# Graph attention on one core: gathered rows that carry their own ones, runs of seven chunks, three scratch writes

## The chip, the cores and the metric

The kernel runs on one core of a Trainium2 chip. The metric is the device time of one launch in microseconds; for the kernel before it is 7131.07 us, the median of three runs (7125.32 to 7133.75). Five engines work side by side and meet at semaphores: PE (matrix products), DVE (VectorE, elementwise work and reductions), ACT (ScalarE, activations and copies), POOL (GpSimd, which here issues the indirect gathers) and SP (SyncE, which issues the plain transfers).

## What is computed

A graph network on 6250 nodes (128 features) and 200,000 edges, sorted by destination `dst`. The destinations are drawn as `6250 * u**2`, so low nodes have many edges and high nodes few. Two convolutions are followed by an attention layer; the part that matters here is the attention:

```python
q = (h @ qw + qb).reshape(n, H, HD)          # H = 8 heads of HD = 16
k = (h @ kw + kb).reshape(n, H, HD)
v = (h @ vw + vb).reshape(n, H, HD)
logits = (q[dst] * k[src]).sum(-1) * scale + (edge_attr @ ew + eb)
amax = segment_max(logits, dst)
pe = exp(logits - amax[dst])
ssum = segment_sum(pe, dst)
w = pe / clip(ssum[dst], 1e-06)
o = segment_sum(w[:, :, None] * v[src], dst)
o = group_norm(o.reshape(n, D) @ ow + ob, an_g, an_b)
return h + o                                  # the caller adds x
```

Each convolution gathers a row for every edge's source, adds a row for its destination and a term of the edge, normalises, applies SiLU, and sums over the destination.

## The kernel before

**Chunks.** The edges are cut into 196 chunks of 1024 (128 partitions by `NT` = 8 columns). All three layers (`conv(1)`, `conv(2)`, and the attention from L1154 on) loop over these chunks with the same driver, `pipeline` (L713). It also writes out, by `in_order` (L701), that DVE, SP, ACT and PE execute in program order; POOL has only its own order.

**The gather.** For each chunk `gather` (L620) issues eight indirect DMAs on POOL (L622), one for each column of 128 edges. In a convolution a row is 128 floats of `b_d`; in the attention it is `KV` = 256 floats of `kv_d` (L39), k and then v, in DRAM. After the eight gathers of a chunk come `REST[i]` writes of a scratch tile `nst2` on POOL (L634): three in a convolution, four in the attention (L28). The next chunk's gathers are ordered behind the last of these writes.

**One attention step, n.** `fetch(n+1)` (L1305) issues the loads and gathers of chunk n+1 into a buffer `g` from a pool of `G + 3` = 11. `second` (L1328) finishes one earlier chunk: it builds the one-hot matrix on DVE (`onehot`, L637), adds the sums of a chunk before (`add_late`, L1292), forms weighted v (`weighted`, L1239: ACT copies `pe` to a seventeenth column behind each head of a tile `v`, DVE multiplies v by `pe`), lets ACT put the maxima `wl` and an end flag `ef` behind it (L1346, L1347), and lets PE sum by destination (`sums`, L1248). Then `first(n)` (L1315) multiplies the gathered k by q (`logits`, L1182; L1187 is the DVE instruction that waits for the gather), and `products` (L1312) lets PE make q for chunk n+1.

**Runs.** The maxima over edges of one destination are found for a run of `G` = 8 chunks at once (`maxima`, L1205): PE transposes, DVE scans twice forward over 512 columns (L1219) and once backward over 1024 (L1222), PE transposes back, DVE subtracts (L1230) and ACT makes `pe`. `spread` (L327) cuts the 196 chunks into runs: the last three have 6, 4 and 2 chunks, the first takes the remainder, all others have `G`. That is 26 runs before. A chunk's `second` comes after its run's maxima, so a chunk lives for a whole run and a little more in its `g` buffer.

**Finishing nodes between chunks.** `plan_batches` (L352) fixes the steps at which a batch of four windows of 128 nodes is finished while the chunks go on (`attention_nodes`, L870), at most 40 of the 49 windows (`NWD` = 40). For each planned step it notes a chunk number, three less than the seconds done so far; on the chip the windows already closed at that chunk are read from the first destination of the chunk (`batches`, L377). The end of each batch is the smaller of the last end plus four and that number of windows. What of the 40 windows is not reached by the last batch is done after the pipeline in `mend` (L643): `to_mend` (L405) makes the count of batches `(43 - last) >> 2`, and a loop around two inner loops runs if it is above zero. `last_nodes` (L935) then does windows 40 to 48.

**Where k and v come from.** In the second convolution `conv_nodes` (L804) writes k and v of four windows to `kv_d` by one DVE addition each (L861) and one transfer each (L858).

Of the kernel before, what the change touches and what calls it, by code (L numbers as in the profile page):

```python
# [8 lines left out]
FP = mybir.dt.float32  # L9
# [3 lines left out]
ALU = mybir.AluOpType  # L13
# [8 lines left out]
P = 128  # L22
D = 128
H = 8
HD = 16
NT = 8
CH = NT * P
REST = {1: 3, 2: 3, 3: 4}  # L28
G = 8
GC = 2  # L30
BN = 4
LG = 2
# [3 lines left out]
DB = D + H  # L36
PITCH = D + 4
VK = H * (HD + 1)
KV = 2 * D  # L39
EPS = 1e-5  # L40
BIG = 1e30
PAD_DST = 1 << 20
# [3 lines left out]
def kernel(ctx: ExitStack, tc: tile.TileContext, x, src, dst, eat, w, out):  # L46
# [9 lines left out]
    nc = tc.nc  # L56
# [295 lines left out]
    def plan_batches(i):  # L352

        ends, todo = steps_of(i)
        out, done = [], 0
        for n, now in enumerate(todo):
            done += len(now)
            if n % 8 == (4 if i == 3 else 1) and n > (40 if i == 3 else 80) and n + 6 < NCH \
                    and (i == 3 or n + 5 in ends):
                out.append((n, max(done - 3, 0)))  # L360
        return out if NWD else []

# [441 lines left out]
    def conv_nodes(b, i, w, m, idle=0):  # L804


        at = span(w, m)
        c = b.pool.tile([P, 2, BN], FP, name="n_c")
        if i == 1:
            nc.vector.tensor_scalar(c[:, 0, :m], U[:, at, D], 1.0, None, ALU.max)  # L810
            nc.vector.tensor_scalar(c[:, 1, :m], U[:, at, D], 1.0, None, ALU.min)
            nc.vector.reciprocal(c[:, 0, :m], c[:, 0, :m])
            nc.vector.tensor_copy(cnt[:, :, at], c[:, :, :m])
        else:
            nc.vector.tensor_copy(c[:, :, :m], cnt[:, :, at])
        st = b.tile(m, "x")
        nc.vector.tensor_tensor(st, U[:, at, :D], c[:, 0, :m, None].to_broadcast([P, m, D]), ALU.mult)
        yield
        tT = b.turned(st, m)
        yield  # L820
        o = b.times(tT, m, squares[f"c{i}_w2"])
        yield
        A = b.tile(m, "A")
        for j in range(m):
            nc.vector.scalar_tensor_tensor(
                A[:, j, :], rows[f"c{i}_b2"], c[:, 1, j:j + 1], o[:, j, :], ALU.mult, ALU.add)
        sq = b.squares_of(A, m)
        yield
        nc.vector.tensor_reduce(b.var(), sq, AX.X, ALU.add)
        yield "root"  # L830
        b.scaled(A, m, f"n{i}_g", f"n{i}_b")
        yield
        nc.scalar.activation(A, A, AF.Silu)
        yield
        if i == 1:
            nc.vector.tensor_tensor(A, A, temb[:, None, :].to_broadcast([P, m, D]), ALU.add)
        else:
            nc.vector.tensor_tensor(A, A, h0[:, at, :], ALU.add)
        yield

        for _ in range(idle):
            yield
        if i == 2:
            nc.sync.dma_start(out=rows_of(h2_d, w, m), in_=A)
        tT = b.turned(A, m, "t")
        yield
        if i == 1:
            ends = ((wab[2][:, D:], None, b_d[2]), (wab[2][:, :D], None, a_d[2]))
        else:
            ends = ((qkv_t[:, 1, :], "kb", kv_d[:, :D]), (qkv_t[:, 2, :], "vb", kv_d[:, D:]),  # L850
                    (qkv_t[:, 0, :], "qb", a_d[3]))
        done = None
        for rhs, bias, d_ in ends:
            o = b.times(tT, m, rhs)
            if bias:
                yield
            if done:
                nc.sync.dma_start(out=rows_of(done[0], w, m), in_=done[1])  # L858
            t = b.tile(m, "o")
            if bias:  # L860
                nc.vector.tensor_tensor(t, o, rows[bias][:, None, :].to_broadcast([P, m, D]), ALU.add)  # L861
            else:
                nc.scalar.copy(t, o)
                yield
            done = d_, t
        if bias:
            yield
        nc.sync.dma_start(out=rows_of(done[0], w, m), in_=done[1])
# [291 lines left out]
    with ExitStack() as es:  # L1160
        pool = lambda n, b, **kw: es.enter_context(tc.tile_pool(name=f"{n}a", bufs=b, **kw))
        pools = {"oh": pool("oh", 2), "ps": pool("ps", 1, space=PSUM)}
        gp, wk, vp = pool("gp", G + 3), pool("wk", 2), pool("vp", 1)
        ps_ = pools["ps"]
        iota = ps_.tile([P, D], FP, name="iota")
        nc.vector.tensor_copy(iota, iota_j)
# [71 lines left out]

        def weighted(k):  # L1239

            k.v = vp.tile([P, NT, VK + H + 1], FP, name="v")
            v4 = k.v[:, :, :VK].rearrange("p t (h c) -> p t h c", c=HD + 1)
            nc.scalar.copy(v4[:, :, :, HD], k.pe)
            nc.vector.tensor_tensor(
                v4[:, :, :, :HD], k.g[:, :, D:].rearrange("p t (h c) -> p t h c", c=HD),
                k.pe[:, :, :, None].to_broadcast([P, NT, H, HD]), ALU.mult)

        def sums(k, wide):  # L1248
            k.u = ps_.tile([P, 512], FP, name="u", tag="u", bufs=2)
# [45 lines left out]
        class Stage:  # L1295
            ahead = 1
            sums, late, nb = [], [], None
            lg, j = None, 0

            def __init__(self, bp):  # L1300
                self.bp = bp
# [2 lines left out]

            def fetch(self, c):  # L1305
                k = loads(c, pools, a_d[3], self.ahead)
                k.g = gp.tile([P, NT, KV], FP, name="g")
                gather(k, k.g, kv_d, REST[3])
                k.qe = []
                return k  # L1310

            def products(self, k):  # L1312
# [2 lines left out]
            def first(self, k):  # L1315
                if self.j == 0:
                    self.lg = wk.tile([P, NT, G, H], FP, name="lg")
                logits(k, self.lg[:, :, self.j, :])
                self.j += 1

            def reduce(self, k):
                pass
# [5 lines left out]
            def second(self, run, ks):  # L1328


                pieces = iter(())
                if run:
                    pieces = maxima(run, self.lg, self.nb, self.bp)
                    self.nb, self.j = None, 0
                for n, k in enumerate(ks):
                    mine = pieces if n == len(ks) - 1 else iter(())
                    next(mine, None)
                    onehot(k, pools, iota)
                    next(mine, None)


                    if self.late:
                        add_late(self.late.pop(0))
                    next(mine, None)
                    weighted(k)
                    nc.scalar.copy(k.v[:, :, VK:VK + H], k.wl)  # L1346
                    nc.scalar.copy(k.v[:, :, VK + H], ef[:, k.c * NT:(k.c + 1) * NT])  # L1347
                    sums(k, VK + H + 1)
                    if self.sums:
                        merge_late(self.sums[0])  # L1350
                        self.late.append(self.sums.pop())
                    self.sums.append(k)
                for _ in pieces:
                    pass

            def batch(self, j):
# [17 lines left out]
        def left(k):  # L1374
            lp = pools["left"]
            left_rows(k, pools, a_d[3], "qe", [P, TB, DB], 3)
            k.g = gp.tile([P, NT, KV], FP, name="g")
            gather(k, k.g, kv_d)
            k.qe = []
            products(k, [(k.ohf.rearrange("p t e -> p (t e)"), k.rows), (k.ea, webl)])  # L1380
            lg = lp.tile([P, NT, H], FP, name="l_lg")
            logits(k, lg)
            neg = lp.tile([P, 4, P], FP, name="l_neg")
            part = lp.tile([P, H, 2], FP, name="l_part")
            junk = lp.tile([P, 4, P], FP, name="l_junk")
            for a in range(2):
                nc.vector.tensor_scalar(neg, k.ohf[:, 4 * a:4 * a + 4, :], 1.0, BIG, ALU.subtract, ALU.mult)
                for h in range(H):
                    bc = ps_.tile([P, 4, P], FP, name="l_bc", tag="blk")
                    for t in range(4):  # L1390
                        nc.tensor.transpose(bc[:, t, :], lg[:, 4 * a + t, h:h + 1].to_broadcast([P, P]), ident)
                    nc.vector.tensor_tensor_reduce(
                        junk, bc, neg, 1.0, -BIG, ALU.add, ALU.max, part[:, h, a:a + 1])
            cm = lp.tile([P, H], FP, name="l_cm")
            nc.vector.tensor_reduce(cm, part, AX.X, ALU.max)
            me = ps_.tile([P, NT, H], FP, name="l_me", tag="pe")
            for t in range(NT):
                nc.tensor.matmul(me[:, t, :], lhsT=k.ohf[:, t, :], rhs=cm, start=True, stop=True)
            nc.vector.tensor_tensor(lg, lg, me, ALU.subtract)

            nc.vector.tensor_scalar(lg, lg, 0.0, None, ALU.min)
            k.pe = lp.tile([P, NT, H], FP, name="l_pe")
            nc.scalar.activation(k.pe, lg, AF.Exp)
            weighted(k)
            sums(k, VK)
            tt = t3[:, bass.ds(k.win, 1), :]
            merge(k, M[:, bass.ds(k.win, 1), :], None, cm[:, None, :], 1)
            add(k, tt, 1)
# [43 lines left out]
```

## Time and profile before

| what | value |
|---|---|
| median of the runs | 7131.07 us |
| the profiled execution | 7126.42 us |
| its span, first to last instruction | 7124.6 us |
| granted TensorE clock, mean | 0.723 |
| POOL busy | 5394.0 us (76%) |
| DVE busy | 5144.2 us (72%) |
| PE busy | 3891.3 us (55%) |
| ACT busy | 3308.5 us (46%) |
| attention, first gather | 4669.4 us into the span |
| attention, end of the pipeline on DVE | 7098.6 us |

The profile names a line, an engine and an operation with its output and inputs, a count, the busy time of the group, the mean duration of one, and the idle time of the engine before it with what ended that idle time. Register, branch, semaphore and DMA-issuing instructions are not counted as busy, and a transfer appears as a wait of whoever needs it. The indirect gathers on POOL do show a duration: it is the time that POOL takes to issue one, not the time until it lands.

### The profile page before, as it was taken

What the parts mean: (1) busy time and instruction counts of PE and PEld (TensorE: products, weight loads), DVE (VectorE), ACT (ScalarE), POOL (GpSimd) and SP (SyncE); (2) the same over time, 40 slices, a digit from 0 to 9 for tenths busy, and PEclk for the clock granted to TensorE, in tenths of its full rate; (3) what the DMA queues carried; (4) which work ended last, traced back from release to release, by engine and by line L of the source; (5) the groups of instructions that cost most, each with busy time, mean ns of one, the idle gap of its engine ahead of it and who ended that gap; (6) DMA issues with size and microseconds to landing.
All of it is one profiled execution on the core that took longest, in us unless ns stands there. A gap on an engine that the chain in (4) does not pass through costs nothing. (4 is left out here: it accounts for less than half of the span.)

```text
span 7124.6 us, 74065 instructions
## 1 busy us (share of the span) xinstructions
PE 3891.3 (55%) x20957; PEld 3685.5 (52%) x20958; DVE 5144.2 (72%) x7564; ACT 3308.5 (46%) x5293; POOL 5394.0 (76%) x6678
## 2 busy tenths in 40 slices
PE   5555555555555455555555555545555555555555
PEld 4555555555555455555555555535555555555554
DVE  7777777777777576667777777736667777777778
ACT  5555555555555555555555555522223333333332
POOL 5777777777777677777777777767777777777774
PEclk7776677777777666666777777767777777777777
DMA  5433333333333333333333333344455555555553
GB/s 148 117 97 91 94 110 92 100 100 100 95 100 89 91 90 94 95 94 89 101 107 106 100 106 106 86 130 132 131 146 140 141 142 140 141 146 141 138 139 89
DMA packets 414321, 800.44 MB, mean 112 GB/s; under 512 B 101813, under 2 KB 274984, under 8 KB 379496
## 3 DMA queue, kind: packets, MB, share of 16 engines
q0 software_dynamic: 175616, 411.34, 22.2%
q1 hardware_dynamic: 232646, 380.69, 19.0%
q10 hardware_dynamic: 5632, 3.51, 0.2%
q8 instruction: 172, 2.82, 0.2%
q14 instruction: 255, 2.09, 0.1%
HBM read 754.19 MB, written 40.96 MB: 112 GB/s over the span
## 5 line engine op out<-in xcount | busy, mean ns | idle before, releaser
L622 POOL DMA_INDIRECT g<-b_d,src_i x3136 | 3000.7, 957 | 978.7 <-issue 940.0
L1030 PE MATMUL u<-h,oh 128*128 128x129 f32 (+1 forms) x6272 | 1395.6, 412 | 1891.2 <-ACT h L1025 1891.2
L1030 PEld LDWEIGHTS u<-h,oh 128*128 128x128 f32 x6272 | 1290.1, 314 | 1971.5 <-ACT h L1025 1963.9
L622 POOL DMA_INDIRECT g<-kv_d,src_i x1568 | 1532.4, 977 | 500.9 <-issue 468.8
L1251 PE MATMUL u<-v,oh 128*128 128x145 f32 x3136 | 750.0, 425 | 767.2 <-DVE nm L1284 765.6
L1251 PEld LDWEIGHTS u<-v,oh 128*128 128x128 f32 x3136 | 698.5, 308 | 801.9 <-issue 801.9
L1000 PE MATMUL m<-pk,ohT 117*128 117x128 f32 x6272 | 973.7, 321 | 134.9 <-DVE h L1006 101.1
L1006 DVE TENSOR_TENSOR h<-m,g 128x1024 f32<-128x1024 f32 x392 | 479.0, 1222 | 762.3 <-DMA g<-b_d,src_i 750.4
L1000 PEld LDWEIGHTS m<-pk,ohT 117*128 117x128 f32 x6272 | 942.0, 237 | 162.1 <-DVE h L1006 126.9
L1025 ACT ACTIVATE h<-h 128x1024 f32<-128x1024 f32 x392 | 414.2, 1057 | 1182.9 <-DVE h L1024 1182.9
L634 POOL MEMSET nst<- 128x392 f32 x1960 | 842.7, 430 | 79.3
L1008 ACT ACTIVATE sq<-h 128x1024 f32<-128x1024 f32 x392 | 413.9, 1056 | 653.8 <-DVE h L1006 650.8
L1009 DVE TENSOR_REDUCE var<-sq 128x64 f32<-128x1024 f32 x392 | 477.7, 1219 | 314.8 <-ACT sq L1008 312.2
L1187 DVE TENSOR_TENSOR g<-qe,g 128x384 f32<-128x384 f32 (+1 forms) x588 | 293.8, 511 | 549.7 <-DMA g<-kv_d,src_i 510.1
L615 ACT ACTIVATE ohT<-ohT,minus_p 112x1024 f32<-112x1024 f32 x588 | 669.9, 1139 | 16.2 <-DMA ohT<-rel_d 16.0
L616 ACT ACTIVATE ohT<-ohT 112x1024 f32<-112x1024 f32 x588 | 621.4, 1057 | 18.7
L1178 PE MATMUL qe<-pk,ohT 117*128 117x136 f32 x3136 | 512.8, 319 | 165.5 <-ACT ebs L1188 159.3
L1178 PEld LDWEIGHTS qe<-pk,ohT 117*128 117x128 f32 x3136 | 474.1, 225 | 198.8 <-ACT ebs L1188 192.3
L1023 DVE TENSOR_TENSOR h<-h,cps 128x1024 f32<-128x1024 f32 x392 | 478.4, 1220 | 13.5
L1024 DVE TENSOR_TENSOR h<-h,cps 128x1024 f32<-128x1024 f32 x392 | 478.4, 1220 | 13.4
L1020 DVE TENSOR_TENSOR h<-h,cps 128x1024 f32<-128x1024 f32 x392 | 475.3, 1212 | 5.9
L639 DVE TENSOR_TENSOR oh<-cps,dm 128x1024 f32<-128x1024 f32 x392 | 475.9, 1214 | 0.0
(265 smaller groups left out, 4383.9 us busy)
## 6 DMA issues: line engine op xcount, KB each, us to landing
ohT<-rel_d SPq DMA_DIRECT2D x294, 896.0 KB
g<-b_d,src_i POOLq DMA_INDIRECT x3136
pk<-a_d SPq DMA_DIRECT2D x588, 56.0 KB
g<-kv_d,src_i POOLq DMA_INDIRECT x1568
ohT<-in_eat_dram SPq DMA_DIRECT2D x294, 40.0 KB
a_d<-n_o SPq DMA_DIRECT2D x28, 256.0 KB
kv_d<-n_o SPq DMA_DIRECT2D x28, 256.0 KB
n_h<-h_d SPq DMA_DIRECT2D x19, 256.0 KB
```

Of the source, the lines that this page charges most:

```text
L615: nc.scalar.activation(k.ohT[:WN, :], k.ohT[:WN, :], AF.Square, bias=minus_p[:WN])
L616: nc.scalar.activation(k.ohT[:WN, :], k.ohT[:WN, :], AF.Relu, bias=1.0, scale=-4.0)
L622: return nc.gpsimd.indirect_dma_start(out=g[:, t, :table_d.shape[1]], out_offset=None, in_=table_d, in_offset=bass.IndirectOffsetOnAxis(ap ...
L634: last = nc.gpsimd.memset(nst2, 0.0)
L1000: nc.tensor.matmul(k.m[:, t, :], lhsT=lhs[:, t * P:(t + 1) * P], rhs=rhs, start=(j == 0), stop=(j == len(terms) - 1))
L1006: nc.vector.tensor_tensor(k.mt, k.m, k.g, ALU.add)
L1009: return lambda: nc.vector.tensor_reduce(var[:, j * NT * H:(j + 1) * NT * H], sq.rearrange("p t (g c) -> p (t g) c", c=HD), AX.X, ALU.add)
L1023: nc.vector.tensor_tensor(k.mt, k.mt, over_edges(gam), ALU.mult)
L1024: nc.vector.tensor_tensor(k.mt, k.mt, over_edges(bet), ALU.add)
L1030: nc.tensor.matmul(k.u[:, :wide], lhsT=k.oh[:, t, :], rhs=k.h[:, t, :wide], start=(t == 0), stop=(t == NT - 1))
L1178: nc.tensor.matmul(qe[:, t, :], lhsT=lhs[:, e], rhs=rhs, start=(j == 0), stop=(j == len(terms) - 1))
L1251: nc.tensor.matmul(k.u[:, :wide], lhsT=k.oh[:, t, :], rhs=k.v[:, t, :wide], start=(t == 0), stop=(t == NT - 1))
```

## The change

Five things are done together.

- `KV` becomes 128 + 136: a row of `kv_d` holds k and then, for each head, 16 values of v and a one. `conv_nodes` writes the v half from a tile `n_v` of 136 columns, with a memset for the ones and one DVE addition for each window in place of one for all.
- `weighted` multiplies these 136 columns by `pe` inside the gathered tile `g`, which has nine columns more for `wl` and `ef`. The separate tile `v` and ACT's copy of `pe` go, and ACT puts `ef` in place when the chunk is fetched.
- Runs have 7 chunks in place of 8 (30 runs in place of 26), and the pool of `g` has `G + 4`, which is again 11.
- The attention's scratch writes go from four to three for each chunk.
- The last part of `maxima` (subtraction, `exp`, `wl`) moves behind the logits of the step (`rest`), the second forward scan and the backward one move behind `sums`, and a batch starts three steps after the end of a run, 20 batches in place of 19.

```diff
-REST = {1: 3, 2: 3, 3: 4}
-G = 8
+REST = {1: 3, 2: 3, 3: 3}
+G = 7
-KV = 2 * D
+KV = D + VK
@@ plan_batches
-            if n % 8 == (4 if i == 3 else 1) and n > (40 if i == 3 else 80) and n + 6 < NCH \
-                    and (i == 3 or n + 5 in ends):
+            if n > (40 if i == 3 else 80) and n + 6 < NCH and (
+                    n - 3 in ends and n + 3 not in ends if i == 3 else n % 8 == 1 and n + 5 in ends):
                 out.append((n, max(done - 3, 0)))
@@ conv_nodes
+            if bias == "vb":
+                t = b.pool.tile([P, BN, VK], FP, name="n_v")[:, :m, :]
+                v4 = t.rearrange("p w (h c) -> p w h c", c=HD + 1)
+                nc.vector.memset(v4[:, :, :, HD], 1.0)
+                for j in range(m):
+                    nc.vector.tensor_tensor(
+                        v4[:, j, :, :HD], o[:, j, :].rearrange("p (h c) -> p h c", c=HD),
+                        rows[bias].rearrange("p (h c) -> p h c", c=HD), ALU.add)
+                done = d_, t
+                continue
@@ attention
-        gp, wk, vp = pool("gp", G + 3), pool("wk", 2), pool("vp", 1)
+        gp, wk, vp = pool("gp", G + 4), pool("wk", 2), pool("vp", 1)
@@ weighted
-            k.v = vp.tile([P, NT, VK + H + 1], FP, name="v")
+            k.v = k.g[:, :, D:]
             v4 = k.v[:, :, :VK].rearrange("p t (h c) -> p t h c", c=HD + 1)
-            nc.scalar.copy(v4[:, :, :, HD], k.pe)
             nc.vector.tensor_tensor(
-                v4[:, :, :, :HD], k.g[:, :, D:].rearrange("p t (h c) -> p t h c", c=HD),
-                k.pe[:, :, :, None].to_broadcast([P, NT, H, HD]), ALU.mult)
+                v4, v4, k.pe[:, :, :, None].to_broadcast([P, NT, H, HD + 1]), ALU.mult)
@@ fetch
-                k.g = gp.tile([P, NT, KV], FP, name="g")
+                k.g = gp.tile([P, NT, KV + H + 1], FP, name="g")
                 gather(k, k.g, kv_d, REST[3])
                 k.qe = []
+                nc.scalar.copy(k.g[:, :, KV + H], ef[:, c * NT:(c + 1) * NT])
@@ Stage.first
                 logits(k, self.lg[:, :, self.j, :])
                 self.j += 1
+                self.rest()
@@ Stage.second
                     next(mine, None)
                     onehot(k, pools, iota)
-                    next(mine, None)
                     if self.late:
                         add_late(self.late.pop(0))
                     next(mine, None)
                     weighted(k)
                     nc.scalar.copy(k.v[:, :, VK:VK + H], k.wl)
-                    nc.scalar.copy(k.v[:, :, VK + H], ef[:, k.c * NT:(k.c + 1) * NT])
                     sums(k, VK + H + 1)
+                    next(mine, None)
...
-                for _ in pieces:
+                self.pieces = pieces
+                if run and run[-1].c == NCH - 1:
+                    self.rest()
+
+            def rest(self):
+                for _ in self.pieces:
                     pass
```

More of the change, by code (lines that the diff above doesn't have):

```diff
@@ L1297 @@
             sums, late, nb = [], [], None
-            lg, j = None, 0
+            lg, j, pieces = None, 0, iter(())
             def __init__(self, bp):
@@ L1376, in left @@
             left_rows(k, pools, a_d[3], "qe", [P, TB, DB], 3)
-            k.g = gp.tile([P, NT, KV], FP, name="g")
+            k.g = gp.tile([P, NT, KV + H + 1], FP, name="g")
             gather(k, k.g, kv_d)
```

## The prediction

> **What bounds the kernel now.** I read the page first (POOL 76%, DVE 72% of the span: no verdict), then the attention alone by groups, then the waits, then the order of time on POOL. The change lies almost wholly in the attention, from 4669 to 7099 us. The groups of that stretch, then DVE's waits from 4700 to 7040 us:
>
> ```profile
> L622 POOL DMA_INDIRECT g<-kv_d,src_i x1547 | 1512.5, 978 | 475.8 <-issue 463.0 <-DVE g L1187 5.4 <-DVE wl L1234 4.2
> L634 POOL MEMSET nst<- 128x392 f32 x776 | 333.2, 429 | 33.6
> ```
> ```profile
> DVE g L1187 <- DMA g<-kv_d,src_i: 484.9, 304, 8.6
> ```
>
> POOL's idle time before gathers is 0.30 us each and nearly all "issue": it waits for nobody. DVE waits 485 us for gathers. One chunk of POOL is 8 x (0.978 + 0.30) + 4 x (0.429 + 0.04) = 12.1 us, and 196 of these are 2375 us; the stretch of the gathers, 4669 to 7051, has 2382. So POOL's own instructions set the pace, and the scratch writes are on the path. In order of time, first with three writes (second convolution), then with four:
>
> ```profile
> 4604.38 0.94 POOL L622 DMA_INDIRECT g<-b_d,src_i  x1 [0.30 <-issue]
> 4605.31 1.41 POOL L634 MEMSET nst<- 128x392 f32 x3
> 4607.02 0.95 POOL L622 DMA_INDIRECT g<-b_d,src_i  x1 [0.30 <-issue]
> ```
> ```profile
> 5341.70 0.94 POOL L622 DMA_INDIRECT g<-kv_d,src_i  x1 [0.30 <-issue]
> 5342.64 1.89 POOL L634 MEMSET nst<- 128x392 f32 x4
> 5344.83 0.95 POOL L622 DMA_INDIRECT g<-kv_d,src_i  x1 [0.30 <-issue]
> ...
> 5352.34 2.86 POOL L622 DMA_INDIRECT g<-kv_d,src_i  x1 [0.30 <-issue]
> ```
>
> Three writes take 1.41 us, four 1.89. The last row is a gather three times as long as its neighbours; on DVE the backward scan of a run lies over it:
>
> ```profile
> 5352.15 2.28 DVE L1222 TENSOR_TENSOR_SCAN fw<-nbe,fw 64x1024 f32<-64x1024 bf16 x1
> ```
>
> The gather starts 0.19 us after the scan and ends 0.77 us after it, 1.9 us late. That happens about once in a run.
>
> **DVE's reserve.** Its time not spent waiting for gathers is 2340 - 485 = 1855 us for 192 chunks (the count of L1190 there), 9.65 us a chunk against POOL's 12.1.
>
> **The change, part by part.**
>
> *Fourth write:* 195 gaps between chunks x 0.48 us = **-94 us**, as long as DVE stays below POOL.
>
> *Runs of 7:* 30 runs for 26. Four more backward scans stall a gather by 1.9 us each: **+8 us**. The Trainium skill (SBUF — State Buffer, Who interferes with whom) has two-input DVE instructions contend only with GpSimd instructions that read SBUF, and infers that issuing transfers is spared; that would make this term 0. The row above shows the stall, so I take 8. Since the scans now come later in the step, a stall could also fall on the scratch writes: between -45 (all of the present stalls gone, 24 x 1.9) and +15.
> On DVE a run costs 2.28 + 2 x 1.24 + 0.68 + 8 x 0.21 = 7.1 us whatever its length but for a few tenths: per chunk 0.89 becomes 1.0. A batch costs about 6.9 us (ten instructions of 0.2 to 0.69), one for 7 chunks and not 8: +0.12.
>
> *Weighted v in place:* 1088 elements for 1024, at 1.21 us for 1024 about +0.08 us a chunk. ACT loses the copy of `pe` (0.258 us). DVE's sum is 9.65 + 0.11 + 0.12 + 0.08 = 10.0 us a chunk, against POOL's 12.1 - 0.48 + 0.1 = 11.7. The reserve of 1.7 us hides these; without cover they would cost 0.31 x 196 = 61 us.
>
> *Longer life of `g`:* it is now released by PE's sums, not by `weighted`; a shorter run gives a step back. Chunk c takes the buffer of c - 11, whose second came one step before the fetch and now comes two before. POOL waits for no buffer now and should not afterwards: 0. If it did, all eight gathers of the chunk and the writes behind them would queue, and DVE's L1187 would wait for them. The `ef` copy moves ahead in ACT's order, past the copies of the earlier chunks; it waits for the same release, two steps old: 0. If it instead waited for the gather landing in the same tile, `compared` and the copies of `wl` behind it would wait, and PE's sums with them. Against that, ACT's L1346 (columns 136 to 143 of `v`) starts at 7058.65 while DVE's write of the other columns only starts at 7058.85: columns of one tile are not ordered.
>
> *Longer rows:* 1056 bytes for 1024. POOL's price for a gather is the unknown that matters. Both ends from one view, attention then convolution (512-byte rows):
>
> ```profile
> L622 POOL DMA_INDIRECT g<-kv_d,src_i x1539: 942/946/2936, 4699.2 to 7038.0; - x193
> ```
> ```profile
> L622 POOL DMA_INDIRECT g<-b_d,src_i x3025: 938/944/2424, 199.9 to 4599.4; - x190
> ```
>
> Doubling the bytes added 2 ns to the median; 32 more add nothing on this row. The other end is a row cut in two, which could double the issue: +0.95 us. I take 0. The transfer: the Trainium skill (DMA: Bandwidth & Descriptors, How a descriptor splits into AXI transactions) says that a piece of HBM not starting on 256 bytes is fetched from the boundary below. 1024 bytes are 32 beats; 1056 at a pitch of 1056 are 33 to 40, on average an estimated 36.5, 14% more. This rule speaks against the change: the gathers' queue has 31.9% of engine time from 5300 to 7000 us, so 4.5% of 2382 us, 107 us, if that were the path. The row says it isn't (DMA share 0.51 in all): 0, and some tenths on the last landing.
>
> *k and v rows in the second convolution:* one addition of 0.68 us becomes a memset and four of about 0.27 (the 128-wide rows of L825). The 10 batches lie under POOL there, too. The three groups at its end don't: 0.2 + 3 x 0.27 - 0.56 = 0.45 each, +1.4 us. The tail of the attention saves the 1.1 us that L1244 waits for ACT's copy. Together **+1 us** with the longer multiplications.
>
> *Batches and `mend`:* what is late next. By the rule of the plan, the old last batch starts at step 188 and looks at chunk 179. With dst = 6250 u² over 200,000 sorted edges, its first edge is at u = 179 x 1024 / 200,000 = 0.916, node 5250, window 41: capped at 40, nothing is left. The new last batch starts at 180 (step 187 fails, as a run ends at 190) and looks at chunk 170: u = 0.870, node 4735, window 36. Hence (43 - 36) >> 2 = 1: the loop of `mend`, skipped now, runs one batch, with nothing beside it. Its price is not in this trace. The batch alone, from the rows of the attention's batches: DVE 0.20 + 0.35 + 0.69, PE 1.06, ACT 0.59, PE 1.05, DVE 0.68, ACT 0.63, DVE 0.68, ACT with its table load 1.60, DVE 0.35 + 0.69 + 2 x 0.69 + 0.69 + 0.69 = 12.0, the store about 3 until landed: 15 us. Passing one loop is seen once here:
>
> ```profile
> 7098.14 0.44 DVE L1276 TENSOR_TENSOR flat<-flat,u 128x272 f32 x1
> 7103.27 0.36 DVE L874 TENSOR_SCALAR n_rec<-flat 128x24 f32<-128x24 f32 x3 [4.70 <-DMA n_h<-h_d]
> ```
>
> 4.7 us. The taken path passes the skipped inner loop, the batch loop's end and the outer loop's end beside that: 2 to 6 passages, 9 to 28 us. I take 18, between the ends because the loop's end must also await its transfers: **+33 us**, bounds 24 to 43.
>
> Also one more batch under POOL, +1. Sum: -94 + 8 + 1 + 33 + 1 = **-51 us**: the span goes from 7124.6 to about 7074, the profiled execution from 7126.4 to 7075. The median lies 4.7 us above that execution: 7131 - 51 = **7080 us**.
>
> **The rivals.**
>
> *The DVE becomes the bound.* Runs of 7 bring a step of maxima or of a batch oftener, and a step of maxima takes some 16 us. Were the chain of waits to need the whole 11.7 us and 0.2 more, POOL would wait for buffers and the gain would be 94 - 0.2 x 196 = 55: 7080 + 39 = 7119. For it: DVE has no gap over a tenth in steps with maxima. Against: 1.7 us of reserve a chunk.
>
> *The gather gets dearer* (the slower side). One mechanism: L622's issue grows with the odd row length. Each 0.1 us costs 1568 x 0.1 = 157 us: 7237. It decides from 51 / 1568 = 33 ns a gather. For it: rows are no longer a power of two, and no such gather is in the trace. Against: 944 and 946 ns.
>
> *The change does more than I count:* the scans' stalls fall on the writes and `mend` costs 24: 7080 - 53 - 9 = 7018; half of the stalls gone, 7050.
>
> **How the numbers follow.** Likeliest, POOL bound with `mend`: 0.70, 7055 to 7105. Stalls gone or `mend` cheap: 0.09. DVE bound: 0.10, 7105 to 7130. Dearer gather: 0.11. The range 7048 to 7112 holds the first, most of half-gone stalls, and a little of the DVE case. A measurement of this kernel can tell about 0.2%, 14 us, from no change: faster (below 7117) 0.85, same 0.04, slower 0.11.
>
> **What would show it.** Right: POOL's triples of writes take 1.41 us in the attention, gathers stay at 946 ns median, 30 long gathers beside L1222, DVE's waits for gathers fall from 2.5 to about 1.7 us a chunk, and between the last `add_late` and `last_nodes` a lone batch of L874 to L907 takes some 33 us. Wrong: gathers whose idle time ends with PE u or DVE v (buffers), a median above 980 ns, or no lone batch.

## The result, and the profile after

The changed kernel takes **7053.03 us** (median of 4 runs, 7051.68 to 7058.71), the kernel before beside it 7130.90 (7125.32 to 7133.75): a ratio of 0.9893, 95% interval 0.9876 to 0.991. That is 78 us less by the medians and 73.3 by the spans of the two profiled executions (7124.6 and 7051.3). Forecast were 51.

Where the 73.3 us went is read from five moments in each trace:

| moment, us into the span | before | after | stage's change |
|---|---|---|---|
| first gather of the attention | 4669.4 | 4666.6 | -2.8 |
| last gather of the attention | 7050.1 | 6960.6 | -86.7 |
| end of the pipeline on DVE | 7098.6 | 7004.7 | -4.4 |
| first instruction of `last_nodes` | 7103.3 | 7028.9 | +19.5 |
| end of the span | 7124.6 | 7051.3 | +1.1 |

The gathers' stretch first. The gather is now L623, the write L635, the instruction that waits for the gather L1198. The groups of the attention (busy us, mean ns, idle time before them and what ended it), then DVE's wait for gathers from 4700 to 6930 us:

```profile
L623 POOL DMA_INDIRECT g<-kv_d,src_i x1568 | 1522.4, 971 | 519.1 <-issue 472.2 <-PE u L1261 24.1 <-ACT ebs L1199 8.0
L635 POOL MEMSET nst<- 128x392 f32 x588 | 253.4, 431 | 22.6
```
```profile
DVE g L1198 <- DMA g<-kv_d,src_i: 368.5, 180, 7.3
```

588 writes are three for each of 196 chunks. A gather issues as fast as before (its median is 947 ns). DVE still waits for gathers, 368.5 us in 190 chunks, 1.9 a chunk against 2.5: POOL still sets the pace. New is the end of the first row: PE and ACT now end some of POOL's idle time. In order of time on POOL:

```profile
5340.95 1.40 POOL L635 MEMSET nst<- 128x392 f32 x3
5342.74 0.95 POOL L623 DMA_INDIRECT g<-kv_d,src_i  x1 [0.39 <-issue]
...
5354.23 0.95 POOL L623 DMA_INDIRECT g<-kv_d,src_i  x1 [0.39 <-issue]
5355.49 2.38 POOL L623 DMA_INDIRECT g<-kv_d,src_i  x1 [0.31 <-issue]
```

The triple takes 1.40 us in place of 1.89, but the gather behind it starts after 0.39 us, not 0.30. Gather to gather across a chunk's end the median went from 3.13 to 2.74 us, 0.39 less and not 0.48. The last row is a gather held up by the backward scan, which is L1233 here and runs from 5354.83 to 5357.11: the gather ends 0.76 us after it.

Where the time before a chunk's first gather comes from is seen at the start of the attention, where the first eleven chunks take fresh buffers. The last such chunk and one of the next two, before and then after:

```profile
4787.92 0.95 POOL L622 DMA_INDIRECT g<-kv_d,src_i  x1 [0.16 <-issue]
...
4799.81 0.95 POOL L622 DMA_INDIRECT g<-kv_d,src_i  x1 [0.30 <-issue]
```
```profile
4781.00 0.95 POOL L623 DMA_INDIRECT g<-kv_d,src_i  x1 [0.15 <-issue]
...
4805.17 0.95 POOL L623 DMA_INDIRECT g<-kv_d,src_i  x1 [0.39 <-issue]
```

A fresh buffer costs the same in both kernels. From the twelfth chunk on POOL must ask whether a used one is free, and this costs 0.14 us before and 0.24 after.

Second, the end. DVE between the last `add_late` (L1286) and `last_nodes` (the last row):

```profile
7004.30 0.44 DVE L1286 TENSOR_TENSOR flat<-flat,u 128x272 f32 x1
7011.56 0.18 DVE L885 TENSOR_SCALAR n_rec<-flat 128x32 f32 x1 [6.82 <-DMA n_xr<-in_x_dram]
...
7023.35 0.69 DVE L913 TENSOR_TENSOR n_A<-n_A,n_xr 128x512 f32<-128x512 f32 x1
7028.85 0.35 DVE L885 TENSOR_SCALAR n_rec<-flat 128x24 f32<-128x24 f32 x3 [4.81 <-issue]
```

This is the lone batch that the prediction expected, with 6.8 us to enter the loop, 12.5 of work and 4.8 to leave.

### The profile page after: what moved, and what is told of

It reads as the page before. It is cut to its first block, busy times and chain, and to the rows that moved or that the text cites. A ratio compares the mean times of both kernels' runs of the same rounds, so it can differ in the third digit from the quotient of the medians.

```text
span 7051.3 us, 75298 instructions
## 1 busy us (share of the span) xinstructions
PE 3858.6 (55%) x21045; PEld 3643.6 (52%) x21046; DVE 5182.3 (73%) x7700; ACT 3300.5 (47%) x5111; POOL 5296.6 (75%) x6482
## 5 line engine op out<-in xcount | busy, mean ns | idle before, releaser
L623 POOL DMA_INDIRECT g<-b_d,src_i x3136 | 2996.0, 955 | 977.8 <-issue 942.4
L623 POOL DMA_INDIRECT g<-kv_d,src_i x1568 | 1522.4, 971 | 519.1 <-issue 472.2
L1261 PE MATMUL u<-g,oh 128*128 128x145 f32 x3136 | 694.3, 402 | 666.5 <-issue 640.6
L1261 PEld LDWEIGHTS u<-g,oh 128*128 128x128 f32 x3136 | 645.1, 287 | 709.7 <-issue 701.8
L635 POOL MEMSET nst<- 128x392 f32 x1764 | 760.1, 431 | 68.0
L1019 ACT ACTIVATE sq<-h 128x1024 f32<-128x1024 f32 x392 | 413.8, 1056 | 646.5 <-DVE h L1017 641.9
L1198 DVE TENSOR_TENSOR g<-qe,g 128x384 f32<-128x384 f32 (+1 forms) x588 | 285.0, 511 | 431.3 <-DMA g<-kv_d,src_i 396.6
L1034 DVE TENSOR_TENSOR h<-h,cps 128x1024 f32<-128x1024 f32 x392 | 478.4, 1221 | 13.5
```

Source lines behind the costliest of these rows:

```text
L623: return nc.gpsimd.indirect_dma_start(out=g[:, t, :table_d.shape[1]], out_offset=None, in_=table_d, in_offset=bass.IndirectOffsetOnAxis(ap ...
L635: last = nc.gpsimd.memset(nst2, 0.0)
L1034: nc.vector.tensor_tensor(k.mt, k.mt, over_edges(gam), ALU.mult)
L1261: nc.tensor.matmul(k.u[:, :wide], lhsT=k.oh[:, t, :], rhs=k.v[:, t, :wide], start=(t == 0), stop=(t == NT - 1))
```

## The experiments

**Theory.** POOL's own instructions set the pace before and after. The dropped write is worth nearly the whole gain, and the rest of the change adds or takes a few tens of microseconds where nothing lies beside it. **Rival.** The write alone can't be dropped: with runs of 8 and the old step, DVE and PE have no reserve, and it is the other parts that let POOL run at the shorter pitch.

Three jobs of four kernels were run, each on one chip and beside the kernel before. In the first job the kernel before took 7333.74 us (7313.71 to 7371.33, 23 runs) at a granted clock of 0.69 to 0.70, in the second and third 7130.54 and 7130.57 us at 0.72 to 0.73. The first and the third ran on a chip of the same number, so it isn't known whether another chip or another condition of the same one made the first job slow. Its times are compared only within it; those of the other two may stand side by side.

### First job: four parts, under the slower condition

*The longer rows alone.* The kernel before with rows of 1056 bytes, written in `conv_nodes` as in the change; tile `v` stays.

```diff
-KV = 2 * D
+KV = D + VK
...
-                v4[:, :, :, :HD], k.g[:, :, D:].rearrange("p t (h c) -> p t h c", c=HD),
+                v4[:, :, :, :HD], k.g[:, :, D:].rearrange("p t (h c) -> p t h c", c=HD + 1)[:, :, :, :HD],
```

> The kernel before with rows of 1056 bytes alone: v stands in the row with a one behind each head, but the tile v, ACT's copy of pe, runs of 8 and four writes stay. Theory (the issue of a gather doesn't depend on the length of the row, and the transfer is hidden): within 5 us of 7131, gathers at a median of 946 ns, the share of the gathers' queue up from 31.9% to about 36%. Rival (the odd row length has a price that the rest of the change hides): 20 us or more above 7131, from 13 ns a gather on.

Measured: 7340.90 us (12 runs), ratio 0.9996 (0.9979 to 1.0014); median gather 949 ns. The row length costs nothing that can be seen. The rival of a dearer gather is out. The gap across a chunk's end is 3.14 us, as before (3.13), so the longer rows are not what lengthened POOL's start of a chunk either.

*The fourth write back in the changed kernel.*

```diff
-REST = {1: 3, 2: 3, 3: 3}
+REST = {1: 3, 2: 3, 3: 4}
```

> The kernel after with the fourth scratch write put back in the attention, nothing else. Theory: a pitch of about 12.0 us a chunk by the median (11.51 + 0.49), so +90 us against after, 7053 to about 7140, and no better than before: all of the gain hangs on the one write. Rival (rows, order and shorter runs bring a part of the gain by themselves): below 7110.

Measured: 7356.19 us (10 runs), ratio 1.0033 (1.0016 to 1.005). With four writes the changed kernel is a little slower than the kernel before: its other parts together gain nothing. Its gap across a chunk's end is 3.22 us for 3.14 in the kernel of the rows alone: the dearer asking is there with four writes, too.

*The fourth write dropped from the kernel before, nothing else.*

```diff
-REST = {1: 3, 2: 3, 3: 4}
+REST = {1: 3, 2: 3, 3: 3}
```

> The kernel before with one edit: three scratch writes a chunk in the attention and not four; runs of 8, tile v and rows of 1024 bytes stay. Theory (POOL's own instructions set the pace, a write costs 0.49 us of POOL in each of 195 gaps): about -94 us, 7130 to 7037, with POOL's pitch of a chunk at a median of 11.40 us, so faster than the whole change. Rival (the shorter runs and the step of lead are what make a third write's removal possible; with runs of 8 DVE or the buffers hold POOL back): -40 us or less, and POOL's idle time before gathers ends with a DVE instruction.

Measured: 7478.50 us (4 runs), ratio **1.0191** (1.0163 to 1.022). Slower: under this condition the theory falls. Its waits from 4700 to 6900 us:

```profile
ACT v L1243 <- remote: 211.8, 70, 7.2
POOL g L622 <- DVE cm L1287: 199.2, 43, 8.4
DVE fw L1219 <- remote: 104.7, 18, 10.5
```

POOL now waits for DVE, 43 times and up to 8.4 us, and DVE and ACT wait for something that the profile can put down to no instruction or transfer of the core ("remote"). One such place, just after PE's transposes of a run:

```profile
5284.92 0.28 PE L1216 MATMUL lt<-ident,lg 128*64 128x128 f32 x1 [1.14 <-issue]
...
5289.48 1.21 DVE L1219 TENSOR_TENSOR_SCAN fw<-nbs,lt 64x512 f32<-64x512 bf16 x1 [5.68 <-remote]
```

Four such transposes take 1.06 us together at 5290.75, for the next half. Here the last of them ends, by the trace (which models the ends of PE's products), at 5285.2, and the scan that reads them starts 4.3 us later.

*The lone batch taken away from the changed kernel*, by last runs of 5, 4 and 2 chunks, so that the plan reaches window 40.

```diff
-        sizes, n = ([2, 4, 6], G) if i == 3 else ([1, 1], GC)
+        sizes, n = ([2, 4, 5], G) if i == 3 else ([1, 1], GC)
```

> The kernel after with the last three runs of 5, 4 and 2 chunks in place of 6, 4 and 2. The steps at which nodes are finished move, the last one starts at step 188 and reaches window 40, so the loop after the pipeline is passed over. Theory (the lone batch costs 24.1 - 4.7 = 19.4 us): 7053 to about 7033. Rival (the time of the lone batch is moved into the end of the pipeline, where DVE has no cover after the last gather): within 6 us of 7053.

Measured: 7287.64 us (6 runs), ratio 0.9916 (0.9893 to 0.9939). `mend` takes 3.0 us, but from the last gather to the end of the pipeline there are 78.5 us, for 43.6 in the changed kernel with four writes. That work of the lone batch moved there isn't shown: the kernel before with three writes, whose last runs are as they were, has 90.9 us there in this job. The changed kernel itself was not in it.

### Second job: which part does it

Four kernels, all with three writes: runs of 8 or of 7 (with their plan of batches and buffers), each with the old step (tile `v`, old order of the pieces) and the new one.

*The changed kernel again:*

> The changed kernel once more, to stand beside the other runs of this job on one chip. Expected: ratio 0.989 to the kernel before, attention pitch 11.5 us median, lone batch of mend 24 us. If this chip has the matrix products held up as on the chip of the earlier experiments, and that makes PE and DVE late, the rival expects it nearer to 1.0.

*The old step with runs of 8* is the kernel with the write dropped, once more:

> The kernel before with three writes in place of four, repeated. Theory A (runs of 8 leave PE and DVE no reserve at the shorter pitch; that is a property of the kernel): again slower than the kernel before or equal, 1.00 to 1.02, with gaps of over 3.5 us between chunks where POOL waits for buffers. Rival C (only the held-up matrix products of that one chip did it): about -90 us, ratio 0.987, gaps of 2.64 us and POOL waiting for nobody.

*The old step with runs of 7:*

```diff
-REST = {1: 3, 2: 3, 3: 4}
-G = 8
+REST = {1: 3, 2: 3, 3: 3}
+G = 7
...
-            if n % 8 == (4 if i == 3 else 1) and n > (40 if i == 3 else 80) and n + 6 < NCH \
-                    and (i == 3 or n + 5 in ends):
+            if n > (40 if i == 3 else 80) and n + 6 < NCH and (
+                    n - 3 in ends and n + 3 not in ends if i == 3 else n % 8 == 1 and n + 5 in ends):
...
-        gp, wk, vp = pool("gp", G + 3), pool("wk", 2), pool("vp", 1)
+        gp, wk, vp = pool("gp", G + 4), pool("wk", 2), pool("vp", 1)
```

> The kernel before with runs of 7, their plan of batches and three writes, but with the separate tile for weighted v and the old order inside a step. Theory A (the run length gives the reserve): like the changed kernel, ratio 0.989 to 0.992, with the lone batch of mend. Rival B (the weighting in place and the moved pieces give the reserve): like the kernel before with three writes alone.

*The new step with runs of 8:* the last two of these edits backwards and `G = 8`, in the changed kernel.

> The changed kernel with runs of 8 and the old plan of batches (no lone batch in mend), 11 buffers as in both kernels. Theory A: like the kernel before with three writes alone, POOL waits for buffers, ratio 1.00 or above. Rival B: pitch 11.5 us, and with the 20 us of mend gone about -95 us, ratio 0.987.

Measured, medians of 4 runs each, the kernel before 7130.54 (7 runs):

| three writes | runs of 8 | runs of 7 |
|---|---|---|
| old step | 7032.09 us, 0.9858 (0.9842 to 0.9875) | 7052.10 us, 0.9889 (0.9872 to 0.9905) |
| new step | 7028.16 us, 0.9853 (0.9836 to 0.9869) | 7055.88 us, 0.9895 (0.9879 to 0.9912) |

In this job the write alone brings 98 us and beats the changed kernel by 24. Runs of 7 cost 20 with the old step and 28 with the new one. In both pairs of profiles the lone batch in `mend` is 20 us of this (24 to 25 us for 4 to 5); with the new step the stalled gathers add 13 us (long ones delayed by 26 us for 13). The new step makes no difference that the intervals can tell; with runs of 8 its profile shows why: about 17 us more of asking for buffers, and 21 us less of stalled gathers (13 for 35). A and B of the expectations both had the kernel with only the write dropped no faster, and fall with that; that the old step with runs of 7 comes near the number of A and the new step with runs of 8 near that of B speaks for neither, as POOL sets the pace in all four. C holds: the write's removal lost only under the condition of the first job. No wait of these four kernels is "remote". In the kernel with the write dropped, DVE's wait from 4700 to 6930 us is

```profile
DVE g L1187 <- DMA g<-kv_d,src_i: 398.6, 261, 6.8
```

so even with runs of 8 POOL sets the pace, and DVE has 2.1 us a chunk to spare.

The pairs also show what the asking for a buffer consists of. Semaphore instructions of POOL's sequencer (POOLq) at the gather, old step then new step, both with runs of 8:

```profile
L622 POOLq EVENT_SEMAPHORE  x579: 17/17/43, 54.1 to 6945.3; - x193
```
```profile
L622 POOLq EVENT_SEMAPHORE  x764: 17/17/43, 54.1 to 6945.8; - x191
```

The new step has 185 more, one for each chunk from the twelfth on, and the gap across a chunk's end is 2.739 us in both kernels with the new step and 2.648 in both with the old one. A buffer `g` that PE reads last and ACT writes into has more releasers to be asked than one that DVE alone uses. Whether PE's reading or ACT's writing brings the second wait was not tried apart.

### Third job: the lone batch, the scan, and one write more

*The last runs of 5, 4 and 2 again:*

> The changed kernel with last runs of 5, 4 and 2 chunks, so that the plan reaches the last window and mend has nothing to do, repeated beside the others. Theory: mend's 20 us are saved, 7055 becomes 7036, ratio 0.987 to the kernel before, with the tail behind the last gather still near 45 us. Rival: the work moves into the tail, as on the chip of the first try: tail 60 to 80 us, total 7050 or more.

Measured: 7038.59 us (4 runs), ratio 0.9869 (0.9853 to 0.9886). `mend` 2.8 us, the tail 47.6 (44.1 and 43.1 in the two profiles of the changed kernel). Here the lone batch is a cost that can be had back: 14 to 17 us against the two medians of the changed kernel.

*The scan.* The kernel before with three writes, without the two lines of the backward scan; it leaves out that part of the maxima, so what follows works on other values, with the same instructions.

```diff
-            nc.vector.tensor_tensor_scan(
-                fw[:q, ::-1], nb["nbe"][:q, ::-1], fw[:q, ::-1], -BIG, ALU.add, ALU.max)
```

> The kernel before with three writes and without the backward scan, so it leaves out that part of the maxima. Theory (the scan holds up the issue of a gather): no long gathers at all, and 24 x 1.5 us = 35 us less than with three writes alone, 6997 us, ratio 0.981. Rival (issue is spared by DVE's scans, the long gathers have another cause): some 24 long gathers stay, and nothing changes, 7032 us, since DVE is not the bound.

Measured: 6995.87 us (4 runs), ratio 0.9812 (0.9796 to 0.9829), 36 us below the same kernel with the scan. Gathers with the scan, then without (shortest/median/longest ns):

```profile
L622 POOL DMA_INDIRECT g<-kv_d,src_i x1568: 942/946/2987, 4673.9 to 6956.7; - x196
```
```profile
L622 POOL DMA_INDIRECT g<-kv_d,src_i x1568: 942/946/1462, 4668.9 to 6916.0; - x196
```

24 gathers of over 1.6 us became none, and all delays over the median fell from 46 to 11 us, which is 35 of the 36. So DVE's scan does hold up the issue of an indirect transfer. The traces show how: in every kernel of this study each gather of the attention over 1.6 us began while a backward scan ran and ended 0.75 to 0.78 us after it, whenever it had begun; a gather already under way keeps its time (957 ns at most), and so does a scratch write (452 ns at most).

The scan is not the only one. In the kernel without it:

```profile
5345.06 0.69 DVE L793 TENSOR_TENSOR n_A<-n_A,n_rs 128x512 f32<-128x512 f32 x1
5345.11 1.46 POOL L622 DMA_INDIRECT g<-kv_d,src_i  x1 [0.30 <-issue]
```

In all fourteen traces every gather of the attention between 1.0 and 1.6 us that no backward scan holds up began during such an operation of a batch on `n_A` or `n_x`, or (three times) during the sum of `l3` and `ebs`, and ended about 0.82 us after it. What these share with the backward scan is that both inputs lie in SBUF, by the program; that this is the cause was not tested by moving one. Under operations with an input in PSUM no gather is late: in the kernel before 183 began during the one-hot comparison (L639, `iota` in PSUM) and 178 during the multiplication by `pe` (L1244, `pe` in PSUM), 1.2 us each, and none took more than 955 ns. The batches' share is small, 10.9 us of delay before and 10.2 after.

From the new step with runs of 8:

```profile
5245.81 0.96 POOL L622 DMA_INDIRECT g<-kv_d,src_i  x1 [0.30 <-issue]
5246.10 2.28 DVE L1232 TENSOR_TENSOR_SCAN fw<-nbe,fw 64x1024 f32<-64x1024 bf16 x1
5246.77 1.40 POOL L634 MEMSET nst<- 128x392 f32 x3
```

In that trace the scan starts during a chunk's last gather and lies over the writes: all keep their time. That kernel has 8 long gathers of 26 scans, the old step with runs of 8 has 24.

*One write more dropped*, in the changed kernel and in the new step with runs of 8:

```diff
-REST = {1: 3, 2: 3, 3: 3}
+REST = {1: 3, 2: 3, 3: 2}
```

> The changed kernel with two writes in place of three. DVE still waits 1.9 us a chunk for gathers in the changed kernel. Theory: that reserve covers one more write, POOL's median pitch falls by 0.48 to 11.02 us, and 195 of these are -94, ratio 0.977. Rival: three writes are the last that can be dropped, DVE and PE are then the bound, POOL waits for buffers, ratio 0.99 or above.

> The changed kernel with runs of 8, the old plan of batches and two writes. If the length of the runs gives no reserve that this pitch needs: 94 us below the same with three writes, 7028 - 94 = 6934 us, ratio 0.973, and below the changed kernel with two writes by the 20 us of the lone batch. Rival A (runs of 8 run out of reserve first, at a shorter pitch): POOL waits for buffers once in a run, ratio above that of the changed kernel with two writes.

Measured: with runs of 7 6973.98 us (4 runs), ratio 0.9779 (0.9762 to 0.9795); with runs of 8 **6959.91 us** (4 runs), ratio 0.9761 (0.9745 to 0.9778), the fastest whole kernel of the study. None with fewer than two writes was run. The gap across a chunk's end is 2.257 us in both, again 0.482 less. DVE's wait in the first, from 4700 to 6860 us:

```profile
DVE g L1198 <- DMA g<-kv_d,src_i: 304.3, 121, 6.9
```

That is 1.6 us for each of 192 chunks, so the bound is still POOL. With runs of 7 the second write brought 79 to 82 us and not 94; some 7 us of the rest are the tail, 50.0 us for 43 to 44. With runs of 8 the second write brought 68 us and not 94: the scans, which lay over the writes, now meet 24 gathers, not 8 (31 us for 13 of delay), and the tail is 52.8 us for 46.5.

## Why the prediction came out as it did

**The bound and the sign: right.** POOL's instructions set the pace, outside the first job. The rows that were to show it did: triples of 1.40 us, a median gather of 947 ns, a lone batch. Of the 30 long gathers named there were 18. DVE's wait is 1.9 us a chunk where 1.7 was named.

**Fourth write, -94: the instruction right, the sum too large.** A write is 0.482 us in each of three comparisons. But the change got 195 x 0.39 = -76 from it.

**Longer life of `g`, 0: this is the term that ate the rest, +18.** The prediction asked only whether POOL would find its buffer still taken. It did not, but asking costs: 195 x 0.09 us for the added semaphore (17 us for the 185 chunks that ask). The rows that could have warned were in the trace before: 0.16 us ahead of the gather into the last fresh buffer, 0.30 ahead of the next, though POOL waits for nobody in either. So asking already had a price, and the change gave the buffer to two more engines.

**Four more stalls, +8: wrong in sign, inside its bounds of -45 and +15.** The step that failed is "four more backward scans stall a gather". 30 scans made 18 gathers longer than 1.6 us, where 26 before had made 24; all delays of gathers over the median sum to 39 us for 50. That is the -11 between -76 and the -87 of the stretch. The mechanism was right, as the run without the scan shows. That a scan over the writes is free had been named as the lower bound, and this is what happened to some: 36 writes lay under a backward scan, where 4 did before. Against the Trainium skill's inference that issuing is spared (SBUF — State Buffer, Who interferes with whom), the trace was the better guide; its other half, that an instruction which only writes isn't held up, is what the writes show.

**`mend`, +33: mis-sized, +19.5.** Its lower bound, 24, was too high. The batch took 12.5 us for an estimated 15. The rows listed for it add up to 11.3 us, not to the 12.0 written, and the product with `w_ow` took 2.07 us where 1.05 was counted. The 3 us for the store are not among the 12.5; whether some of them lie in the 4.8 us that it took to leave, the rows don't show. Entering and leaving took 11.6 us less the 4.7 paid before anyway, +6.9 where 18 was taken "between the ends". That is 1.5 passages of the one kind that the trace showed, below the 2 to 6 that were bounded.

**Tail and rows, +1: -4 and -3.** The tail's 4 us are within what it varies by (43.1 to 54.2 us in the kernels with three writes outside the first job); the convolutions' 3 us are scatter, too, as their last gather lies between 4609.7 and 4624.0 in the ten profiles outside the first job.

**Longer rows, 0: right for the time.** From 5300 to 6800 us the gathers' queue has 31.9% of 16 engines' time for 985 gathers before and 35.8% for 1024 after: 8% more a gather, where 14% was estimated, and hidden behind POOL's own instructions.

**Sum.** -76 - 11 - 4 + 19.5 + 1 - 3 is -73.5, against -73.3 by the spans. The forecast of -51 lies as near as it does because errors opposed each other: it charged the stalls 19 us and `mend` 13.5 too much, and left out the 18 of the added semaphore; 8 more are the tail and scatter. The 7053 us lie just below the 7055 to 7105 called likeliest, 5 us above the lower end of the range; that they lie inside owes something to luck.

**DVE as the bound: refuted outside the first job, not in it.** With two writes DVE still waits for POOL. In the first job the kernel before with three writes became slower by 1.9%, and there POOL waited for DVE, which had waits of its own that no row of the trace explains.

**Still open.** In the first job "remote" waits from 4700 to 6900 us sum to 12.5 us in the kernel before with longer rows, 29 in the changed kernel with four writes, 242 in the one with three and the last runs shortened, and 485 in the kernel before with three; in all kernels outside it, to none. Under that condition three writes with the change's other parts and the shortened last runs gain (0.9916) where the write alone loses (1.0191). Which part makes this difference was not tried. What the condition is, is not settled either: in the convolutions such waits were there in all four kernels, 951 to 1011 us, at a granted clock of 0.69 to 0.70 over the span for 0.72 to 0.74. In the kernel before with three writes over nine tenths of them stand before an instruction that reads a product of PE or writes the tile `v`, which PE read last, which points to late ends of PE's products; neither that nor a reason is shown.

## What to carry to other kernels

When one engine's own instructions set the pace, an instruction dropped from it is worth its duration times its count, and the other edits of a change are judged by what they add to that engine and to stretches with nothing beside them, a wait for one more engine on each round included. Try the smallest part alone: here it was faster than the whole. And try it in more than one job before calling a reserve safe.

## What was not expected of the hardware

- A gather's issue on POOL, begun under the backward scan, doesn't end until 0.75 us after it or later (but for three in the study that began within 0.04 us of its start); under a batch's operation of 0.69 us with both inputs in SBUF it ends about 0.82 us after that. The forward scans, which read one input from PSUM, held up none: gathers begun under one alone took 968 ns at most.
- Asking for a buffer that is long free costs POOL 0.14 us before a chunk's first gather where DVE alone used the buffer, and 0.24 where PE and ACT did, too.
- One job ran the same kernel 2.8% slower (7333.74 for 7130.5 us), steadily over its 23 runs, with waits of up to 15.6 us that no row of the trace ends.
